# Moving LayerNorm, factor and block-sum steps inside a graph's turn, with shorter GpSimd chains for norms and scales

## The chip, the cores and the metric

The kernel runs on one core of a Trainium2 chip. The core has a matrix engine (TensorE, PE in the profile; its weight loads are PEld), a vector engine (VectorE, DVE), an activation engine (ScalarE, ACT), a general engine (GpSimd, POOL), and a queue that issues transfers (SyncE, SP). Each engine carries out its instructions in the order in which they were issued to it, and waits on semaphores for the others. TensorE's results go into PSUM, which the kernel uses as eight banks of 128 x 512 float32.

The metric is the device time of one execution in microseconds (us), median over the runs.

## The reference

64 graphs of 256 nodes with 256 features each, `x`, and a 256 x 256 adjacency with self loops, `adj`. Two layers, everything in float32:

```python
# layer 0
h   = relu(bn2(conv17(relu(bn1(conv1(x.T))))) + x.T).T    # along the nodes: a 1-tap and a 17-tap convolution
s   = x @ w_se.T + b_se                                   # 3 numbers for each node
A   = exp(-(|s_n|^2 + |s_m|^2 - 2 s_n.s_m)) * adj
nmp = A @ relu(x @ w_msg.T + b_msg)
gi, gh = concat(h, nmp) @ w_ih.T + b_ih, x @ w_hh.T + b_hh
r, z = sigmoid(gi_r + gh_r), sigmoid(gi_z + gh_z)
n   = tanh(gi_n + r * gh_n)
x   = layernorm(x + (1 - z) * n + z * x)
# layer 1
h   = layernorm(x) * gamma + beta
x   = layernorm(x + x + relu(adj @ h @ W_rel + b_rel + h @ W_root))
```

## The kernel before, in words

**Two streams of work.** The 17-tap convolution is done for eight graphs at once (a batch; eight batches) as a polynomial product in a transformed domain. Almost all of it is VectorE butterflies on one large buffer `XF` (lines 105, 302, 304, 362, 466), with 256-column products on TensorE between (`ps_k`, line 385) and, at the start of a batch, transposes and the 1-tap convolution (`ps_xTc`, `ps_c1`). It is written as a Python generator, `conv(b)`. The rest is done graph by graph: one pass of the inner loop, called a turn here, works on graph `k` and, for stages that run ahead or behind, on its neighbours.

**The order is written out by hand.** Nothing reorders instructions: the order of the calls is the order on every engine. At ten points of each turn `pump()` issues a portion of the *next* batch's convolution, in proportion to the number of points passed. So the convolution's VectorE and TensorE instructions lie between the turn's own. The last batch has no convolution beside it.

**A turn for graph k before the change**, in order, `|` being a pump:

- `gates` step 1: `ps_a` (block product 0) copied by ScalarE to `g00` (line 668), `ps_d` (product 1) added by VectorE (L671), a bias added by GpSimd (L672) |
- step 2: `ps_b` (product 4) copied by ScalarE to `g11` (L676), `ps_c` (product 6) added (L679); then ScalarE's last step for the `y` of graph k-2 (L793) and its store |
- `transposes_h(k-1)`: TensorE transposes `h` (L752), ScalarE copies to `hT` with gamma and beta (L754) |
- step 3: product 5 accumulates on `ps_a`, VectorE adds it (L682), GpSimd adds `g01` to `g11` (L684); the loads for later graphs |
- step 4: product 2 on `ps_b`, VectorE adds (L687), ScalarE tanh (L689); `passing(k+1)`: `ps_nmp`, copied by ScalarE (L630) |
- step 5: product 3 on `ps_c`, VectorE adds (L692), ScalarE tanh (L693); GpSimd `sums` for graph k+1 (below); `factors(k+2)`: TensorE transposes `st` (`ps_sT`, L604), ScalarE writes `lr` (L606, L607); `gates_n`: `ps_n`, added by VectorE (L704) |
- `project(k-1)`: `ps_out` from `hT` (L765), copied to `hr` (L766); `update` step 1: the two `gn` operations on VectorE, tanh (L717) |
- `distances(k+2)`: `ps_dist` from `lr` (L616), exp into `AT` (L618); `update` step 2: three VectorE operations on `x`, statistics (L708, L709), and a GpSimd chain for scale and shift (`q`, `sh`, L729 to L734, with a power of -1/2) |
- `messages(k+3)`: `ps_msg` (L584), two VectorE additions for each half (L586 into `st`, L588 into `msg`), ScalarE relu (L589), a GpSimd chain for the squared norms (L593 to L597); `update` step 3: ScalarE writes `h` and `x1` (L740, four instructions) |
- `mask(k+2)` (L621), `aggregate(k-1)` (L777, L779), VectorE statistics of `y`, a GpSimd chain (L787 to L790) |

**Block products.** The gates are one Strassen-like product of 2 x 2 blocks with seven products. Three left sides take part, `nmp`, `x` and `xc` (the convolution's output); each needs four 128 x 128 sums and differences, which `blocks` issues on GpSimd (L638 to L641). For the first graph of a batch the `xc` sums can only be issued when the whole convolution of that batch has been: they stand behind the loop over the eight graphs.

**Buffers.** `g`, `gn`, `h`, `hT`, `lr` and the sums have one buffer each, `AT`, `msg`, `nmp` and `y` two, `x` three, `xT` and `adj` four. PSUM banks go round through all eight, convolution and turn together.

Of the kernel before, what the change touches and what calls it, by code (L numbers as in the profile page):

```python
# [12 lines left out]
F32 = mybir.dt.float32  # L13
AF = mybir.ActivationFunctionType
ALU = mybir.AluOpType
# [14 lines left out]
BG = 8  # L30
# [47 lines left out]
def gnn_two_layers(  # L78
# [498 lines left out]
    def messages(k):  # L577
        MSG[k] = work.tile([P, C, D], F32, tag="msg", name="msg")
        st = sts[k % len(sts)]
        twice = st.rearrange("p m (r e) -> p m r e", e=SR)  # L580
        for m in range(C):
            ps = bank("ps_msg")
            for c in range(C):
                nc.tensor.matmul(ps[:, :D + 4], XT[k][:, c, m * P:(m + 1) * P], wms[:, c, :],  # L584
                                 start=(c == 0), stop=(c == C - 1))
            nc.vector.tensor_add(twice[:, m, :, 0:3], ps[:, D:D + 3].unsqueeze(1).to_broadcast([P, 2, 3]),  # L586
                                 bse_row.unsqueeze(1).to_broadcast([P, 2, 3]))
            nc.vector.tensor_add(MSG[k][:, m, :], ps[:, :D], bmsg)  # L588
# [43 lines left out]

    def blocks(src, s1, s2, s3, s4):

        a11, a12, a21, a22 = (src[:, c, n * P:(n + 1) * P] for n in range(C) for c in range(C))
        nc.gpsimd.tensor_add(s1, a21, a22)  # L638
        nc.gpsimd.tensor_sub(s2, s1, a11)
        nc.gpsimd.tensor_sub(s3, a11, a21)  # L640
        nc.gpsimd.tensor_sub(s4, a12, s2)  # L641
        return a11, a12, s4, a22, s1, s2, s3

    def sums(k, name):
# [8 lines left out]
        LEFT[k, name] = blocks(src, t[:, 0, :], t[:, 1, :], s3, t[:, 2, :])  # L653
# [57 lines left out]
    def update(k):  # L711

        g, w, nn = G[k], XG[k], GN[k]
        parts = nn.rearrange("p n (h e) -> p n h e", h=2)
        stt(nn, g[:, :, 0, :2 * P], 1.0, nn, op0=ALU.add, op1=ALU.mult)
        stt(parts, parts, 0.5, g[:, :, :, 2 * P:])
        nc.scalar.activation(nn, nn, AF.Tanh)  # L717
        yield

        nc.vector.tensor_sub(w, w, nn)  # L720
        stt(w, g[:, :, 1, :2 * P], 3.0, w, op0=ALU.add, op1=ALU.mult)
        stt(w, nn, 4.0, w)
# [12 lines left out]
        yield  # L735

        H[k] = work.tile([P, C, D], F32, tag="h", name="h", bufs=1)
        for i, dst in ((1, H[k]), (0, w)):
            for n in range(C):
                nc.scalar.activation(dst[:, n, :], w[:, n, :], AF.Identity,  # L740
                                     bias=sh[:, i, n:n + 1], scale=q[:, i, n:n + 1])
        X1[k] = w
        yield
# [60 lines left out]
    with tc.tile_pool(name="first", bufs=1) as first_pool:  # L804
# [34 lines left out]
                nc.sync.dma_start(out=t, in_=rows[:, src + at:src + at + n].to_broadcast([P, n]))  # L839
        bn_ = const.tile([P, D], F32)  # L840
        nc.sync.dma_start(out=bn_, in_=rows[:, R_HH + 2 * D:R_HH + 3 * D].to_broadcast([P, D]))
        gb = const.tile([P, 2, C], F32)
        nc.sync.dma_start(out=gb, in_=rows[:, R_GAMMA:R_GAMMA + 2 * D].rearrange("o (v c p) -> p (o v) c", p=P, c=C))

# [12 lines left out]
        nc.vector.tensor_add(bg[:, :, :2 * P], bg[:, :, :2 * P], bhh)  # L857
        nc.gpsimd.tensor_scalar(wrr, wrr, 0.5, None, ALU.mult)
        nc.gpsimd.tensor_scalar(brel, brel, 0.5, None, ALU.mult)
        while STAGE.get(0) != "inverse":  # L860
            total += next(first) or 0.0

# [30 lines left out]
            early.pop(0)()  # L893
    for f in early:
        f()
    sums(0, "xc")

    POINTS = 10
    y_left = None
    for b in range(NB):  # L900
        coming = conv(b + 1) if b + 1 < NB else iter(())
        done, at, goal = 0.0, 0, BG * POINTS - 6
# [9 lines left out]

        for k in range(b * BG, (b + 1) * BG):
            ga, up = gates(k), update(k)
            agg = None
# [12 lines left out]
            pump()  # L928
            step(ga)
            if k + 1 < B:  # L930
                passing(k + 1)
            pump()
            step(ga)
            if k + 1 < B:
                sums(k + 1, "x")
                if (k + 1) % BG:
                    sums(k + 1, "xc")
                sums(k + 1, "nmp")
            if k + 2 < B:
                factors(k + 2)  # L940
            gates_n(k)
            pump()
            if k > 0:
                project(k - 1)
            step(up)
            pump()
            if k + 2 < B:
                distances(k + 2)
            step(up)
            pump()  # L950
            if k + 3 < B:
                messages(k + 3)
            step(up)
            pump()
            if k + 2 < B:
                mask(k + 2)
            if k > 0:
# [58 lines left out]
```

## Time and profile before

| | |
|---|---|
| time, median of 3 runs | 2332.06 us (2329.61 to 2332.12) |
| span of the profiled execution | 2327.1 us, mean granted TensorE clock 0.979 |
| TensorE matmuls, busy | 2150.1 us, 92% |
| TensorE weight loads, busy | 1485.2 us, 64% |
| VectorE, busy | 1807.1 us, 78% |
| GpSimd, busy | 1044.0 us, 45% |
| ScalarE, busy | 872.0 us, 37% |

The first 188 us prepare the filters and the first batch's convolution; then come 64 turns. Busy shares are means over the whole span. The page also draws them in 40 slices, one digit for a tenth; the two rows that matter most here, TensorE's and VectorE's, differ strongly from slice to slice. "Idle before" in a group of instructions is the time in which its engine had nothing to do just ahead of them, and "<-" names what ended that. A wait named on an engine costs time only in a stretch in which that engine is the one that is behind.

### The profile page before, as it was taken

Reading aid. Unit: us, or ns where it says so; the run is one execution under the profiler, and the core shown is the slowest. Engines: PE = TensorE matmul, PEld = TensorE weight load, DVE = VectorE, ACT = ScalarE, POOL = GpSimd, SP = SyncE. Lnnn points to the kernel's source line nnn. Section 1 sums busy time; section 2 is a strip of 40 time slices with the busy share of each in tenths; the row PEclk is TensorE's granted clock in tenths of the full one; section 3 lists DMA queues with packets and bytes.
Section 4 is the critical chain, followed back from the end, with each engine's and each line's share of the span. In section 5 each row is a group of like instructions: output and inputs, shape, how many; then the busy total and the mean of one; then the engine's idle time right before and its main releaser. Section 6 shows DMA issues by size and latency. Waiting matters only on the chain.

```text
span 2327.1 us, 25882 instructions
## 1 busy us (share of the span) xinstructions
PE 2150.1 (92%) x8390; PEld 1485.2 (64%) x8390; DVE 1807.1 (78%) x3212; ACT 872.0 (37%) x1809; POOL 1044.0 (45%) x1829
## 2 busy tenths in 40 slices
PE   7877899999999999999999999999899999999997
PEld 4564577656766566665776567765676666766664
DVE  3992999849996699948998399975999579994454
ACT  4513322443235422353234532244323533235443
POOL 1004544537345453544436273453644545364542
PEclk9989999999999999999999999999999999999998
DMA  5543233222522234132332224222341214321110
GB/s 162 169 156 108 69 125 104 89 84 74 166 68 83 89 127 140 61 108 70 124 119 91 77 73 153 79 86 91 108 151 64 90 65 149 118 73 46 41 33 18
DMA packets 213939, 226.77 MB, mean 97 GB/s; under 512 B 22327, under 2 KB 205614, under 8 KB 213806
## 3 DMA queue, kind: packets, MB, share of 16 engines
q1 hardware_dynamic: 191248, 191.14, 25.9%
q10 hardware_dynamic: 22558, 33.99, 4.0%
q8 instruction: 68, 1.11, 0.2%
q14 instruction: 65, 0.53, 0.1%
HBM read 179.22 MB, written 45.88 MB: 97 GB/s over the span
## 4 chain that ended last, share of the span: by engine, by line
PE 42%; DVE 40%; issue 6%; POOL 5%; ACT 3%; DMA 3%; SPq 0%; ACTq 0%; POOLq 0%; DVEq 0%
DVE XF L105 12%; PE ps_k L385 7%; PE ps_c L657 5%; PE ps_b L657 5%; PE ps_a L657 4%; DVE XF L362 4%; PE ps_c L456 4%; DVE x L105 3%; PE ps_n L701 3%; PE ps_nmp L628 3%; DVE bst L708 3%; PE ps_out L765 2%; DVE XF L466 2%; PE ps_out L777 2%; DVE gn L105 2%
## 5 line engine op out<-in xcount | busy, mean ns | idle before, releaser
L105 DVE SCALAR_TENSOR_TENSOR XF<-XF 128x512 f32<-128x512 f32 (+2 forms) x800 | 572.4, 743 | 6.8
L385 PE MATMUL ps_k<-w,XF 128*128 128x256 f32 x1316 | 300.1, 383 | 12.2 <-ACT AT L618 11.6
L385 PEld LDWEIGHTS ps_k<-w,XF 128*128 128x128 f32 x1316 | 248.4, 191 | 61.7 <-ACT AT L618 17.3
L684 POOL TENSOR_TENSOR g<-g 128x384 f32<-128x384 f32 x64 | 79.6, 1243 | 397.6 <-DVE g L682 397.6
L729 POOL TENSOR_SCALAR q<-mv 128x2 f32<-128x2 f32 x64 | 32.2, 504 | 483.2 <-DVE mv L709 483.2
L765 PE MATMUL ps_out<-wrr,hT 128*128 128x512 f32 x512 | 231.8, 596 | 2.1 <-ACT hT L754 2.1
L589 ACT ACTIVATE msg<-msg 128x512 f32<-128x512 f32 x64 | 40.4, 631 | 370.5 <-DVE msg L588 370.5
L765 PEld LDWEIGHTS ps_out<-wrr,hT 128*128 128x128 f32 x512 | 97.8, 191 | 101.1 <-issue 86.5
L689 ACT ACTIVATE g<-g 128x512 f32<-128x512 f32 x64 | 40.5, 633 | 304.5 <-DVE g L687 303.3
L584 PE MATMUL ps_msg<-wms,xT 128*128 128x260 f32 x512 | 136.7, 408 | 8.1 <-DVE XF L401 4.7
L362 DVE TENSOR_TENSOR XF<-XF 128x512 f32<-128x512 f32 (+3 forms) x128 | 134.7, 1074 | 1.8
L456 PE MATMUL ps_c<-xTc,w 128*128 128x512 f32 x256 | 118.3, 605 | 9.7 <-ACT xTc L448 9.7
L628 PE MATMUL ps_nmp<-AT,msg 128*128 128x256 f32 x512 | 122.8, 383 | 1.1 <-DVE AT L621 1.1
L584 PEld LDWEIGHTS ps_msg<-wms,xT 128*128 128x128 f32 x512 | 95.6, 196 | 42.0 <-issue 19.4
L777 PE MATMUL ps_out<-hr,adj 128*128 128x256 f32 x512 | 121.9, 380 | 0.1
L701 PE MATMUL ps_n<-wn,xT 128*128 128x256 f32 x512 | 121.1, 379 | 0.0
L657 PE MATMUL ps_b<-wg,xcsum 128*128 128x384 f32 x256 | 105.1, 492 | 16.9 <-POOL xcsum L638 16.9
L628 PEld LDWEIGHTS ps_nmp<-AT,msg 128*128 128x128 f32 x512 | 98.3, 192 | 28.8 <-issue 1.8
L754 ACT ACTIVATE hT<-ps_hT,gb 128x256 f32<-128x256 f32 x128 | 65.0, 558 | 123.9 <-PE ps_hT L752 110.6
L682 DVE TENSOR_TENSOR g<-ps_a,bg 128x768 f32<-128x768 f32 x64 | 61.0, 952 | 64.8 <-PE ps_a L657 64.8
L657 PE MATMUL ps_b<-wg,nmpsum 128*128 128x384 f32 x256 | 106.1, 497 | 3.6 <-DVE y L779 2.3
L692 DVE TENSOR_TENSOR g<-g,ps_c 128x384 f32<-128x384 f32 x64 | 35.0, 547 | 95.7 <-PE ps_c L657 95.7
(150 smaller groups left out, 4918.5 us busy)
## 6 DMA issues: line engine op xcount, KB each, us to landing
w<-w2m SPq DMA_DIRECT2D x105, 768.0 KB, 4.8
xn<-in_x_dram SPq DMA_DIRECT2D x32, 512.0 KB, 4.6
xt<-xTc ACTq DMA_DIRECT2D x32, 512.0 KB, 4.7
xT<-xt SPq DMA_DIRECT2D x64, 256.0 KB, 3.9
adj<-in_adjT_dram SPq DMA_DIRECT2D x64, 256.0 KB, 2.7
x<-in_x_dram SPq DMA_DIRECT2D x64, 256.0 KB, 2.8
xb<-in_x_dram SPq DMA_DIRECT2D x32, 512.0 KB, 3.8
out_dram<-y ACTq DMA_DIRECT2D x64, 256.0 KB, 2.2
```

What stands on the lines that cost most here:

```text
L105: nc.vector.scalar_tensor_tensor(o, in0, s, in1, op0=op0, op1=op1)
L362: (nc.vector.tensor_add if add else nc.vector.tensor_sub)(sl(o, n), sl(a, n), sl(b, n))
L385: nc.tensor.matmul(ps, X[:, slot, c * P:(c + 1) * P], w(m, c), start=(c == 0), stop=(c == C - 1))
L456: nc.tensor.matmul(ps, w1[:, c, o * P:(o + 1) * P], xTc[:, c, :], start=(c == 0), stop=(c == C - 1))
L584: nc.tensor.matmul(ps[:, :D + 4], XT[k][:, c, m * P:(m + 1) * P], wms[:, c, :], start=(c == 0), stop=(c == C - 1))
L628: nc.tensor.matmul(ps[:, d * N:(d + 1) * N], MSG[k][:, m, d * P:(d + 1) * P], AT[k][:, m, :], start=(m == 0), stop=(m == C - 1))
L657: nc.tensor.matmul(ps[:, :w.shape[-1]], LEFT[k, name][i], w, start=start and j == 0, stop=j == 2, skip_group_check=not start)
L684: nc.gpsimd.tensor_add(g11, g11, g01)
L701: nc.tensor.matmul(ps[:, n * D:(n + 1) * D], XT[k][:, c, n * P:(n + 1) * P], wn[:, c, :], start=(c == 0), stop=(c == C - 1))
L708: nc.vector.bn_stats(st, src)
L765: nc.tensor.matmul(ps, hT[:, c, n * P:(n + 1) * P], wrr[:, c, :], start=(c == 0), stop=(c == C - 1))
L777: nc.tensor.matmul(po, ADJ[k][:, m, n * P:(n + 1) * P], hr[:, m, :], start=False, stop=(m == C - 1), skip_group_check=True)
```

## The change

Four things are changed, and the results stay the same up to rounding:

1. **Squared norms** (`messages`): two small VectorE instructions with an accumulated output give `-|s|^2` directly; of GpSimd's five instructions one is left.
2. **Scales** (`update`): one GpSimd addition of a constant tile `eps2` takes the place of two instructions; a factor goes into gamma once, at the start.
3. **Order in the turn**: `h` and `x1` (`update` step 3) are issued in the next turn, after its gates step 1 (`up_left`); `transposes_h(k-1)` goes from before step 3 to after step 4; `factors(k+2)` from after step 5 to before step 4; the `x` and `xc` sums from after step 5 to after step 4, the `nmp` sums to just behind `passing`, and `passing` and step 5 lie behind one pump more.
4. **Block sums at a batch's start**: the first graph's four `xc` sums are issued on VectorE and not on GpSimd.

```diff
@@ messages
+        ns = work.tile([P, C], F32, tag="ns", name="ns", bufs=3)
+        sq = work.tile([P, C, 3], F32, tag="sq", name="sq")
+        for m in range(C):
+            nc.vector.scalar_tensor_tensor(sq[:, m, :], st[:, m, 0:3], -1.0, st[:, m, 0:3], op0=ALU.mult,
+                                           op1=ALU.mult, accum_out=ns[:, m:m + 1])
         nc.scalar.activation(MSG[k], MSG[k], AF.Relu)
-        sq = work.tile([P, C, 3], F32, tag="sq", name="sq")
-        ns = work.tile([P, C], F32, tag="ns", name="ns", bufs=3)
-        nc.gpsimd.tensor_mul(sq, st[:, :, 0:3], st[:, :, 0:3])
-        nc.gpsimd.tensor_add(ns, sq[:, :, 0], sq[:, :, 1])
-        nc.gpsimd.tensor_add(ns, ns, sq[:, :, 2])
-        nc.gpsimd.tensor_scalar(twice[:, :, :, 3], ns.unsqueeze(2).to_broadcast([P, C, 2]), -0.5, None, ALU.mult)
-        nc.gpsimd.tensor_scalar(ns, ns, -1.0, None, ALU.mult)
+        nc.gpsimd.tensor_scalar(twice[:, :, :, 3], ns.unsqueeze(2).to_broadcast([P, C, 2]), 0.5, None, ALU.mult)
@@ update
-        nc.gpsimd.tensor_scalar(q[:, 0, :], mv[:, :, 1], 4 * EPS, None, ALU.add)
-        nc.gpsimd.tensor_scalar(q[:, 1, :], mv[:, :, 1], 1 + EPS, 4 * EPS * EPS, ALU.mult, ALU.add)
+        nc.gpsimd.tensor_tensor(q, mv[:, :, 1].unsqueeze(1).to_broadcast([P, 2, C]), eps2, ALU.add)
@@ before the loop, and behind each batch
-    sums(0, "xc")
+    sums(0, "xc", nc.vector)
...
-            sums((b + 1) * BG, "xc")
+            sums((b + 1) * BG, "xc", nc.vector)
@@ the turn
             step(ga)
+            step(up_left)
             pump()
             step(ga)
             step(y_left)
             pump()
-            if k > 0:
-                transposes_h(k - 1)
+            step(ga)
             pump()
-            step(ga)
-            load(k + 3)
-            load_adj(k + 2)
-            load_x(k + 1)
-            pump()
-            step(ga)
-            if k + 1 < B:
-                passing(k + 1)
-            pump()
+            if k + 2 < B:
+                factors(k + 2)
             step(ga)
             if k + 1 < B:
                 sums(k + 1, "x")
                 if (k + 1) % BG:
                     sums(k + 1, "xc")
+            load(k + 3)
+            load_adj(k + 2)
+            load_x(k + 1)
+            pump()
+            if k > 0:
+                transposes_h(k - 1)
+            pump()
+            if k + 1 < B:
+                passing(k + 1)
                 sums(k + 1, "nmp")
-            if k + 2 < B:
-                factors(k + 2)
+            step(ga)
             gates_n(k)
             pump()
...
             if k + 3 < B:
                 messages(k + 3)
-            step(up)
             pump()
...
-            y_left = agg
+            y_left, up_left = agg, up
```

More of the change, by code (lines that the diff above doesn't have):

```diff
@@ L630, in passing, with blocks, sums @@
         nc.scalar.copy(NMP[k].rearrange("p c n -> p (c n)"), ps)
-    def blocks(src, s1, s2, s3, s4):
+    def blocks(src, s1, s2, s3, s4, eng):
         a11, a12, a21, a22 = (src[:, c, n * P:(n + 1) * P] for n in range(C) for c in range(C))
[L638 to L641, printed above, removed]
+        eng.tensor_add(s1, a21, a22)
+        eng.tensor_sub(s2, s1, a11)
+        eng.tensor_sub(s3, a11, a21)
+        eng.tensor_sub(s4, a12, s2)
         return a11, a12, s4, a22, s1, s2, s3
-    def sums(k, name):
+    def sums(k, name, eng=None):
         if name == "x":
@@ L652, in sums @@
             s3 = src[:, 0, P:]
-        LEFT[k, name] = blocks(src, t[:, 0, :], t[:, 1, :], s3, t[:, 2, :])
+        LEFT[k, name] = blocks(src, t[:, 0, :], t[:, 1, :], s3, t[:, 2, :], eng or nc.gpsimd)
     def block_product(k, i, ps, start):
@@ L841, in gnn_two_layers @@
         nc.sync.dma_start(out=bn_, in_=rows[:, R_HH + 2 * D:R_HH + 3 * D].to_broadcast([P, D]))
+        eps2 = const.tile([P, 2, C], F32)
+        nc.gpsimd.memset(eps2[:, 0, :], 4 * EPS)
+        nc.gpsimd.memset(eps2[:, 1, :], 4 * EPS * EPS / (1 + EPS))
         gb = const.tile([P, 2, C], F32)
@@ L859, in gnn_two_layers @@
         nc.gpsimd.tensor_scalar(brel, brel, 0.5, None, ALU.mult)
+        nc.gpsimd.tensor_scalar(gb[:, 0, :], gb[:, 0, :], (1 + EPS) ** -0.5, None, ALU.mult)
         while STAGE.get(0) != "inverse":
@@ L895, in gnn_two_layers @@
         f()
-    sums(0, "xc")
+    sums(0, "xc", nc.vector)
     POINTS = 10
-    y_left = None
+    y_left = up_left = None
     for b in range(NB):
@@ L914, in gnn_two_layers @@
             ga, up = gates(k), update(k)
-            agg = None
             step(ga)
+            step(up_left)
             pump()
@@ L956, in gnn_two_layers @@
                 mask(k + 2)
+            agg = None
             if k > 0:
@@ L965, in gnn_two_layers @@
         if b + 1 < NB:
-            sums((b + 1) * BG, "xc")
+            sums((b + 1) * BG, "xc", nc.vector)
+    step(up_left)
     step(y_left)
```

## The prediction

> **What bounds the kernel now.** I read the page's busy shares and slices, then TensorE's waits, then a table of windows with one row for each turn of a batch, then VectorE's waits in a part of it, and last the timeline of one turn. TensorE looks like the bound (92%), but the slices of the two engines move against each other:
>
> ```profile
> PE   7877899999999999999999999999899999999997
> ...
> DVE  3992999849996699948998399975999579994454
> ```
>
> Of TensorE's own waits, longest in total first, these are the ones that the change touches:
>
> ```profile
> engine line waited for: us in total, times, longest us
> PE ps_hT L752 <- ACT h L740: 28.2, 42, 5.5
> PE ps_dist L616 <- ACT lr L607: 25.8, 25, 2.5
> ...
> PE ps_b L657 <- POOL xcsum L638: 16.9, 8, 5.3
> PE ps_a L657 <- ACT g L668: 16.4, 21, 0.8
> ```
>
> Together 87.3 us, 3.7% of the time. Whether they are worth that is read from the second batch (turns 8 to 15), one row a turn: length, then busy time of TensorE, weight loads, VectorE, ScalarE, GpSimd, the granted clock and the DMA.
>
> ```profile
> core 0: us, PE busy (x) PEld busy (x) DVE busy (x) ACT busy (x) POOL busy (x), PEclk, DMA share, GB/s
> 470.60:513.80 43.20, 41.54 (x158) 25.60 (x157) 16.23 (x25) 22.48 (x45) 13.89 (x34) 1.00 0.30 104
> 513.80:541.30 27.50, 24.68 (x94) 16.28 (x93) 26.17 (x39) 9.88 (x21) 19.09 (x28) 1.00 0.12 38
> 541.30:568.90 27.60, 24.67 (x93) 16.28 (x92) 27.12 (x48) 9.88 (x21) 18.72 (x27) 1.00 0.34 115
> 568.90:617.50 48.60, 45.38 (x189) 34.30 (x188) 46.08 (x83) 12.61 (x26) 19.79 (x40) 1.00 0.43 141
> 617.50:658.50 41.00, 39.97 (x165) 29.82 (x164) 37.87 (x73) 10.84 (x24) 15.65 (x27) 1.00 0.43 135
> 658.50:687.00 28.50, 28.30 (x113) 20.10 (x112) 28.05 (x55) 10.49 (x24) 13.85 (x22) 1.00 0.13 38
> 687.00:716.50 29.50, 27.30 (x102) 18.03 (x101) 28.76 (x50) 10.12 (x22) 19.86 (x28) 0.94 0.30 99
> 716.50:744.30 27.80, 26.95 (x118) 18.81 (x116) 15.19 (x33) 16.71 (x37) 11.91 (x25) 1.00 0.23 75
> ```
>
> The first and the last turn are TensorE's: it idles 1.66 and 0.85 us, VectorE 27.0 and 12.6. The six between have VectorE busy for 194.05 of 202.70 us. There TensorE's waits for `h`, `lr` and `g` are only where it stands while VectorE is behind. What holds VectorE in that stretch (window 508 to 721, which takes in the end of the first turn):
>
> ```profile
> engine line waited for: us in total, times, longest us
> DVE gn L704 <- PE ps_n L701: 2.1, 2, 1.4
> DVE XF L466 <- ACT XF L459: 1.8, 1, 1.8
> DVE g L692 <- PE ps_c L657: 1.0, 1, 1.0
> DVE g L687 <- POOL g L684: 0.9, 1, 0.9
> DVE g L671 <- ACT g L668: 0.8, 1, 0.8
> ```
>
> So a batch is two parts in a row. VectorE's runs from the first turn's late `XF` (L466, which waits for TensorE's 1-tap convolution) to the `y` of the seventh; TensorE's from there (its `ps_b` waits 0.6 us for that `y`, L779, for a bank) through the next batch's first turn. The last batch is TensorE's alone: in the window 2100 to 2290 its only listed wait is one of 1.7 us for `xcsum`.
>
> [...] here a 128x128 sum took 0.45 us on GpSimd when undisturbed, and VectorE's 128x256 took 0.41, so with half the columns VectorE should need about 0.28 (0.68 for 512, 0.41 for 256: 0.27 for each 256, and half of that less).
>
> **Part by part.**
>
> *Sums on VectorE at a batch's start.* TensorE waits 5.3 us once and 1.66 us at each of seven batch starts. At 470 to 477 us GpSimd ends the norm chain, the squared norms and the `y` chain at 476.50 before it starts `xcsum` (476.46 to 476.91); TensorE could have begun at 475.31. VectorE ends its statistics at 474.78 and is then idle until 475.58: the first sum ends near 474.78 + 0.28 + 0.3 (norms, below) = 475.4. The wait falls to about 0.1: 7 x 1.5 = 10.5 us. The other three sums delay L671 by some 0.4 us, in a stretch where VectorE has 27 us to spare. At the first turn GpSimd's sums stood behind 128x768 weight sums of 1.8 us each; on VectorE, idle there from 186.7 to 192.7, they stand behind nothing: 5.3 us. The wait of 1.33 us for `nmpsum` just before goes too, as the GpSimd queue loses four small instructions ahead of it (0.19, 0.19, 0.20 and 1.09 us): 1.3 us.
>
> *`h` and `x1` in the next turn.* Four ScalarE instructions of 0.59 us, 2.36 in all, no longer stand before the copy of `g00`. TensorE loses its 16.4 us of waits, and VectorE its 0.8 us at L671 in the fourth turn of a batch and 1.5 in turn 1. Only VectorE's part counts: 7 x 0.8 + 1.5 = 7.1 us. Now `g11`'s copy stands behind them, but its bank is complete 5.4 us after `ps_a` (two products of 2.7), so it isn't late; and GpSimd's `sh` is finished before the next turn's first copy in the saturated turns (520.50 against 522.52).
>
> *Transposes and factors.* `h` and `lr` are ready long before their readers, so the 28.2 and 25.8 us vanish from the list. I count nothing for that in VectorE's turns, because a new wait takes their place: `hT`'s copies now stand behind the tanh of step 4 on ScalarE, which waits for VectorE's L687. In the turn at 513.8 TensorE without waits would reach `ps_out` at about 531; L687 ends near 530.8 by my estimate (one pump earlier than its 532.8), and tanh (0.63) and two copies (1.02) put `hT` at 532.5. TensorE then waits about 1.5 us at `ps_out`, with hr, distances and messages behind it. The bank wait of `ps_hT` for the convolution (`XF` L401, up to 1.9 us in the fourth turn) passes to a later allocation, behind step 3's 1.9 us: TensorE is earlier at that turn's `ps_n`, where VectorE waits 0.7. I take 0.5 us a batch: 3.5. In the fifth turn VectorE's waits for `ps_c` and `ps_n` (1.0 + 1.4) only change shares, for the TensorE work up to `ps_n` is the same. L687 still has one pump between it and L682, so its wait for GpSimd (0.9) shrinks by 0.3 at most, where that pump is longer: 7 x 0.3 = 2.1.
>
> *Shorter GpSimd chains.* L593 to L595, L597 and one of L729/L730 go: mean durations 369 + 328 + 220 + 307 + 259 ns, 95 us of GpSimd over 64 turns, at 45% use and with no reader waiting except as above. Nothing.
>
> *Norms on VectorE.* Two instructions, four with the accumulator reads, for each turn, on the engine that is behind. The nearest rows are L586 (128x6, mean 151 ns, yet the next starts only 0.07 us after it) and L709 (182 ns). Lower end: two starts of 0.07, 0.15 us a turn. Upper end: four of 0.15, 0.6 us. I take 0.3, four starts of 0.07. They lie in VectorE's part 7 times a batch, in 7 batches: 49 x 0.3 = +14.7 us (7.4 to 29.4). In TensorE's turns VectorE's idle time hides them.
>
> Sum: -10.5 - 5.3 - 1.3 - 7.1 - 3.5 - 2.1 + 14.7 = -15.1, so 2332.1 - 15.1 = 2317.0 us.
>
> **Rivals.**
>
> *A, TensorE's waits come off the clock.* For: TensorE is busy for 92% and the four waits are 87.3 us. In full that gives 2244.8. Against: VectorE in its six turns has just 8.65 us to give in a batch. If TensorE's lead took half of that, 7 x 4.3 = 30 us, in place of the 7 x 1.6 that I count, the time would be 2317.0 - 30 + 11.2 = 2298.
>
> *B, the norms eat it all.* For: the added instructions stand on the saturated engine, and the earlier sums let GpSimd's 128x128 operations lie beside more of VectorE's butterflies: in the turn at 513.8 a sum took 1.43 us where it takes 0.45 alone, and butterflies of 128x512, median 0.68, average 0.77. With 0.6 us a turn the sum is -15.1 + 14.7 = -0.4; with 0.2 us a saturated turn of such contention (42 turns) besides, +8: 2340, slower. Against: statistics instructions of like size go by at 0.1 us from start to start (L709 to the next L708).
>
> *C, new waits end the gain.* VectorE's L682 comes one pump earlier after L679; its slack was 1.8 us in the fifth turn. If it waits 1 us in three turns of each batch that is +21 less what later waits shrink by (about half): 2327, no change.
>
> **How the numbers follow.** My forecast 0.55 (2305 to 2327), A in part or in full 0.17, no change through B or C 0.15, slower 0.13. The likeliest gives 2317. From 2297 (A's half) to 2333 (B's upper end and a little contention) leaves out about 0.07 below and 0.11 above. Faster 0.55 + 0.17 = 0.72; same 0.15; slower 0.13.
>
> **What would show it.** Right: `xcsum` gone from TensorE's waits or near 0.1 us; no more waits for `h`, `lr` and `g` L668, but `ps_out` waiting for `hT` with 20 us or more in total; the middle six turns with VectorE's busy share unchanged, and 0.15 to 0.6 us more of it a turn. Wrong: lengths of those six turns falling by over 3 us a batch (then TensorE's lead counted), or growing (then the norms or GpSimd's contention cost more), or TensorE's first turns losing less than 1 us.

## The result, and the profile after

| | before | after |
|---|---|---|
| time, median | 2332.09 us | 2354.65 us (4 runs, 2352.38 to 2354.84) |
| ratio | 1 | 1.0096, 95% interval 1.0079 to 1.0114 |
| span of the profiled execution | 2327.1 us | 2352.7 us |

The changed kernel is slower by 22.6 us, where 15 us of gain was forecast. In its listing the lines from about L600 on are one lower than before (L687 of before is L686, L692 is L691, L765 is L764).

The slices of TensorE and VectorE on the page of after:

```profile
PE   7878899999999999998999999999999999999997
...
DVE  3994999759896799949998499975989679895454
```

The two still change places, so a batch is still VectorE's part and TensorE's part in a row. TensorE's longest waits in after (us in total, times, longest):

```profile
PE ps_out L764 <- ACT hT L753: 56.2, 28, 3.3
PE ps_k L385 <- DVE g L686: 21.3, 14, 1.9
...
PE ps_b L656 <- ACT g L675: 14.4, 21, 1.2
...
PE ps_k L385 <- ACT XF L400: 10.1, 7, 2.1
```

The waits for `h`, for `g` at L668 and for `xcsum` are gone or small, as foreseen, and `ps_out` waits for `hT`, as foreseen. Not foreseen are the wait of `ps_b` for `g` at L675 (the copy of `g11`, which now stands behind `h` and `x1`) and the two of `ps_k`: it waits for a PSUM bank that VectorE's step 4 (L686), or ScalarE's L400, has still to read. The second batch by turns, in the columns of the table shown before:

```profile
core 0: us, PE busy (x) PEld busy (x) DVE busy (x) ACT busy (x) POOL busy (x), PEclk, DMA share, GB/s
467.70:510.40 42.70, 41.56 (x157) 25.77 (x157) 17.18 (x33) 22.63 (x45) 10.82 (x25) 1.00 0.31 105
510.40:537.30 26.90, 24.41 (x93) 16.19 (x92) 25.57 (x43) 9.77 (x21) 18.63 (x23) 1.00 0.12 39
537.30:567.70 30.40, 26.45 (x94) 16.75 (x93) 29.89 (x54) 10.31 (x22) 18.48 (x25) 0.94 0.32 104
567.70:616.50 48.80, 45.66 (x189) 34.20 (x188) 44.84 (x88) 12.38 (x25) 20.31 (x28) 1.00 0.44 141
616.50:661.30 44.80, 41.92 (x165) 30.91 (x165) 38.98 (x78) 11.28 (x24) 13.94 (x22) 0.96 0.39 123
661.30:690.10 28.80, 28.50 (x113) 20.03 (x113) 28.35 (x53) 9.83 (x22) 12.74 (x19) 1.00 0.12 37
690.10:722.10 32.00, 27.58 (x101) 17.49 (x101) 31.19 (x59) 10.94 (x24) 19.21 (x23) 0.95 0.29 98
722.10:748.60 26.50, 26.50 (x117) 18.81 (x116) 14.47 (x33) 16.72 (x37) 10.55 (x19) 1.00 0.22 72
```

The six middle turns grew from 202.70 to 211.70 us. VectorE's busy time in them went from 194.05 to 198.82, its idle time from 8.65 to 12.88: about half of the loss is more work or slower work on VectorE, half is VectorE standing (idle at a wait; such a stretch is called a stand below). It stands in the fifth turn above all (41.0 before, 44.8 now). VectorE's waits in the window 505 to 727 of after:

```profile
engine line waited for: us in total, times, longest us
DVE g L691 <- PE ps_c L656: 5.5, 2, 3.8
DVE gn L703 <- PE ps_n L700: 2.3, 2, 1.2
...
```

Before, L692 waited 1.0 us there. Over the six batches from the second to the seventh the mean lengths of the eight turns, worked out from the two traces at the first `ps_a` product of each turn, are:

| turn of a batch | 1 | 2 | 3 | 4 | 5 | 6 | 7 | 8 | sum |
|---|---|---|---|---|---|---|---|---|---|
| before | 43.9 | 27.2 | 28.3 | 48.1 | 41.0 | 28.5 | 30.3 | 27.2 | 274.5 |
| after | 42.4 | 27.8 | 28.4 | 49.8 | 44.0 | 28.8 | 31.7 | 26.7 | 279.5 |

In these means the six middle turns grow by 7.0 us a batch; VectorE's busy time is 3.9 of that and its idle time 3.1.

### The profile page after: what moved, and what is told of

Its sections match the earlier page's. It is cut to its first block, busy times and chain, and to the rows that moved or that the text cites. A ratio compares the mean times of both kernels' runs of the same rounds, so it can differ in the third digit from the quotient of the medians.

```text
span 2352.7 us, 25793 instructions
## 1 busy us (share of the span) xinstructions
PE 2159.4 (92%) x8390; PEld 1482.5 (63%) x8390; DVE 1845.6 (78%) x3500; ACT 877.3 (37%) x1809; POOL 971.1 (41%) x1480
## 4 chain that ended last, share of the span: by engine, by line
DVE 44%; PE 42%; issue 6%; POOL 3%; DMA 3%; ACT 2%; SPq 0%; ACTq 0%; DVEq 0%; POOLq 0%
DVE XF L105 16%; PE ps_k L385 7%; PE ps_c L656 5%; PE ps_a L656 5%; PE ps_c L456 4%; PE ps_out L764 4%; PE ps_b L656 3%; DVE XF L362 3%; PE ps_n L700 3%; DVE x L105 3%; DVE bst L707 3%; PE ps_nmp L627 3%; DVE XF L466 2%; PE ps_out L776 2%; PE ps_d L656 2%
## 5 line engine op out<-in xcount | busy, mean ns | idle before, releaser
L105 DVE SCALAR_TENSOR_TENSOR XF<-XF 128x512 f32<-128x512 f32 (+2 forms) x800 | 595.8, 773 | 6.5
L385 PE MATMUL ps_k<-w,XF 128*128 128x256 f32 x1316 | 307.9, 388 | 43.1 <-DVE g L686 21.3
L764 PE MATMUL ps_out<-wrr,hT 128*128 128x512 f32 x512 | 256.3, 648 | 56.2 <-ACT hT L753 56.2
L729 POOL TENSOR_TENSOR q<-mv,eps 128x4 f32<-128x4 f32 x64 | 31.3, 489 | 537.5 <-DVE mv L708 293.9
L764 PEld LDWEIGHTS ps_out<-wrr,hT 128*128 128x128 f32 x512 | 103.2, 206 | 178.5 <-issue 96.6
L691 DVE TENSOR_TENSOR g<-g,ps_c 128x384 f32<-128x384 f32 x64 | 35.1, 549 | 174.6 <-PE ps_c L656 174.6
L656 PE MATMUL ps_b<-wg,nmpsum 128*128 128x384 f32 x256 | 106.0, 496 | 16.1 <-ACT g L675 14.4
L792 ACT ACTIVATE y<-y,sh,q 128x256 f32<-128x256 f32 x128 | 69.9, 594 | 134.6 <-POOL sh L789 133.9
L700 PEld LDWEIGHTS ps_n<-wn,xT 128*128 128x128 f32 x512 | 97.3, 190 | 26.9
L776 PEld LDWEIGHTS ps_out<-hr,adj 128*128 128x128 f32 x512 | 96.4, 190 | 15.9 <-ACT hr L765 1.6
```

The lines of the kernel that those rows point to most:

```text
L105: nc.vector.scalar_tensor_tensor(o, in0, s, in1, op0=op0, op1=op1)
L385: nc.tensor.matmul(ps, X[:, slot, c * P:(c + 1) * P], w(m, c), start=(c == 0), stop=(c == C - 1))
L656: nc.tensor.matmul(ps[:, :w.shape[-1]], LEFT[k, name][i], w, start=start and j == 0, stop=j == 2, skip_group_check=not start)
L700: nc.tensor.matmul(ps[:, n * D:(n + 1) * D], XT[k][:, c, n * P:(n + 1) * P], wn[:, c, :], start=(c == 0), stop=(c == C - 1))
L764: nc.tensor.matmul(ps, hT[:, c, n * P:(n + 1) * P], wrr[:, c, :], start=(c == 0), stop=(c == C - 1))
L776: nc.tensor.matmul(po, ADJ[k][:, m, n * P:(n + 1) * P], hr[:, m, :], start=False, stop=(m == C - 1), skip_group_check=True)
```

## The experiments

All ratios are to the kernel before, run beside each on the same chip; one per cent is 23.3 us.

| run | what it is | median us | ratio, 95% interval |
|---|---|---|---|
| e1 | before + new order only | 2374.88 | 1.0183 (1.0167 to 1.0199) |
| e2 | after with the old order | 2309.48 | 0.9903 (0.9888 to 0.9918) |
| e3 | before + transposes and pump moved | 2404.55 | 1.0316 (1.0298 to 1.0334) |
| e4 | after, norms on GpSimd again | 2345.78 | 1.0058 (1.0042 to 1.0075) |
| e5 | before + pump moved | 2360.95 | 1.0119 (1.0104 to 1.0134) |
| e6 | before + transposes moved | 2388.70 | 1.0224 (1.0193 to 1.0254) |
| e7 | before + sums on VectorE | 2310.22 | 0.9899 (0.9884 to 0.9914) |
| e8 | after with the old pumps | 2368.41 | 1.0146 (1.0127 to 1.0165) |
| e9 | e6, bank of `hT` taken early | 2387.42 | 1.0225 (1.0204 to 1.0246) |
| e10 | e6, copies into `hT` before the tanh | 2334.50 | 1.0002 (0.9991 to 1.0013) |
| e11 | after, transposes at the old place | 2338.10 | 1.0019 (1.0007 to 1.0030) |
| e12 | e2 + `h`, `x1` in the next turn | 2316.11 | 0.9923 (0.9907 to 0.9939) |
| e13 | before without GpSimd's sums | 2275.79 | 0.9762 (0.9747 to 0.9777) |
| e14 | e5 without GpSimd's sums | 2291.38 | 0.9824 (0.9811 to 0.9838) |
| e15 | after, copies before the tanh | 2335.21 | 1.0012 (1.0005 to 1.0020) |
| e16 | e8, copies before the tanh | 2333.51 | 1.0006 (0.9999 to 1.0013) |
| e17 | after, `ps_nmp` ahead of the pump | 2333.57 | 1.0000 (0.9992 to 1.0008) |
| e18 | e16, gap filled with repeated products | 2320.37 | 0.9946 (0.9933 to 0.9959) |

**Which part is it? e1, e2, e4, e7.** Theory 1: the order in the turn costs the time. Theory 2: the norms on VectorE cost it.

e1 takes only the turn of the changed kernel, without the other three parts:

```diff
+            step(up_left)
...
-            if k > 0:
-                transposes_h(k - 1)
+            step(ga)
             pump()
-            step(ga)
...
```

> The kernel before with the new order of the turn alone (h and x1 in the next turn, transposes, factors and sums at their new places; norms, scales and the batch-start sums stay on GpSimd). Theory 1 (the order costs it: with one pump more ahead of step 5, the convolution's products stand before a PSUM bank that VectorE's L686 must free, and VectorE then waits for ps_c): 2355 to 2370 us, as the changed kernel but without its gain of some 15 us at the batch starts. Theory 2 (the norms on the saturated VectorE cost it): 2325 to 2335 us.

e2 is its complement, the changed kernel with the turn of before:

```diff
-            if k + 2 < B:
-                factors(k + 2)
...
+            if k > 0:
+                transposes_h(k - 1)
...
```

> The changed kernel with the old order of the turn: norms on VectorE, one GpSimd scale instruction less, batch-start sums on VectorE. Theory 1: 2320 to 2328 us (the batch starts give 15 to 17, the norms cost 0.17 us in 49 turns, 8). Theory 2: 2345 us or more.

e4 puts the five GpSimd instructions for the norms back into the changed kernel:

```diff
-            nc.vector.scalar_tensor_tensor(sq[:, m, :], st[:, m, 0:3], -1.0, st[:, m, 0:3], op0=ALU.mult,
-                                           op1=ALU.mult, accum_out=ns[:, m:m + 1])
+        nc.gpsimd.tensor_mul(sq, st[:, :, 0:3], st[:, :, 0:3])
...
```

> The changed kernel with the squared norms on GpSimd again, as before. Theory 1: 2343 to 2350 us (8 us less than the changed kernel's 2354.7). Theory 2: 2325 to 2335 us.

e7 takes the block sums alone:

```diff
-            sums((b + 1) * BG, "xc")
+            sums((b + 1) * BG, "xc", nc.vector)
```

> The kernel before with the batch-start sums on VectorE and nothing else. Both theories: 2312 to 2318 us, as the waits for xcsum (16.9 us) go. If it is 2310 or less, the norms on VectorE cost the kernel with the old order nothing; at 2301 they cost the 8 us that they cost with the new order.

The order costs 42.7 us (e1), the sums bring 23.6 (e7), the norms cost 8.9 (after against e4, an interval of some 3 to 14 us). Together +28.0 where +22.6 was measured: they add up within their intervals. Theory 1 holds, theory 2 accounts for less than half of the loss. With the old order the norms and shorter chains together change nothing that can be measured (0.9903 against 0.9899).

**Which move of the order? e3, e5, e6, e8, e11, e12.** e5 moves one pump, so that steps 3 and 4 come earlier; e6 moves the transposes behind step 4; e3 does both:

```diff
# e5
             if k > 0:
                 transposes_h(k - 1)
+            step(ga)
             pump()
             step(ga)
             load(k + 3)
...
             pump()
-            step(ga)
+            pump()
             if k + 1 < B:
                 passing(k + 1)
-            pump()
# e6
-            if k > 0:
-                transposes_h(k - 1)
             pump()
...
             step(ga)
+            if k > 0:
+                transposes_h(k - 1)
             if k + 1 < B:
                 passing(k + 1)
```

> The kernel before with one move: step 3 follows step 2 after one pump, and transposes_h with its pump goes behind step 4, so that passing and step 5 lie behind one pump more. Theory 1: this move is the harmful one, 2350 to 2370 us, with waits of ps_k for g L687 in two turns of each batch. Theory 2, or another part of the order at fault: within 5 us of 2332.

> The kernel before with one pump moved: the one between transposes_h and step 3 now stands behind the pump after step 4, ahead of passing and step 5; transposes_h stays ahead of step 3. Theory 1a (the place of the pump does the harm: two portions of the convolution now stand ahead of step 5, their products need the banks of step 3 and 4 back from VectorE, and VectorE later waits for ps_c): 2375 to 2410 us, with 20 us or more of ps_k waiting for g L687. Theory 1b (the place of the transposes does it, through hT's copies behind the tanh): within 6 us of 2332.

> The kernel before with transposes_h moved from before step 3 to after step 4, every pump at its old place. Theory 1a: 2325 to 2338 us. Theory 1b: 2370 us or more, with waits of ps_out for hT.

Each alone costs, the transposes twice as much as the pump (+52 and +28), and both about their sum (+74). The whole new order costs less than these two moves of it (43 us, e1); which of its other moves gives the difference back was not tested. e8 and e11 undo one of the two in the changed kernel (e8 also puts GpSimd's sums back behind step 5), e12 takes `h` and `x1` in the next turn as the only move:

```diff
# e8: pumps as before, transposes behind step 4
+            pump()
             step(ga)
...
# e11: transposes before step 3, pumps as after
+            if k > 0:
+                transposes_h(k - 1)
             step(ga)
             pump()
# e12
+            step(up_left)
...
-            step(up)
```

> The changed kernel with its pumps at their old places: h and x1 in the next turn, factors ahead of step 4, transposes_h after step 4, norms and batch-start sums on VectorE; sums after step 5 as before. Theory 1a: 2300 to 2312 us, below the 2309.5 of the changed kernel with the old order or equal to it. Theory 1b: 2345 us or more.

> The kernel after with nothing but the transposes put back before step 3 (pumps, factors, h and x1, sums, norms as after). If the place of the transposes is the main harm (e6: +55 of order's +43 with the helping moves): 2310 to 2325. If the pump placement is the main harm (e5: +27 by itself): 2335 to 2350.

> All that helps: block sums on VectorE, norms, eps2, and of the turn's order only h and x1 issued in the next turn; transposes, pumps and factors at their old places. My step for h and x1 in the prediction says -7 against e2 (2309.5): 2302. If TensorE's waits for h stand only where VectorE is behind and L671's wait is made up elsewhere: 2308 to 2311. If the later h runs into the transposes before step 3 (TensorE then waits for h at ps_hT with 1 us in each turn): 2315 to 2335.

e8 is slower than the changed kernel itself, so the old pumps do not help while the transposes stand behind step 4. With the transposes back (e11) the changed kernel loses 18 us of its time. The +4 us that are left are fewer than what pump, norms and sums leave by themselves (28 + 9 - 24 = 13). The move of `h` and `x1` brings nothing: e12 stands 0.2% above e2, with intervals that touch.

**What the moved pump costs: e13, e14.** In e5 VectorE's butterflies take longer, although their number is the same. Two of their groups by form, first in the kernel before, then in e5 (busy us, mean ns):

```profile
L105 DVE SCALAR_TENSOR_TENSOR XF<-XF 128x512 f32<-128x512 f32 x448 | 334.3, 771 | 5.0
...
L302 DVE TENSOR_TENSOR XF<-XF 128x256 f32<-128x256 f32 x112 | 46.5, 416 | 0.2
```

```profile
L105 DVE SCALAR_TENSOR_TENSOR XF<-XF 128x512 f32<-128x512 f32 x448 | 350.4, 808 | 5.0
...
L302 DVE TENSOR_TENSOR XF<-XF 128x256 f32<-128x256 f32 x112 | 53.5, 478 | 0.2
```

The changed kernel has the same lengthening:

```profile
L105 DVE SCALAR_TENSOR_TENSOR XF<-XF 128x512 f32<-128x512 f32 x448 | 348.9, 805 | 5.0
```

With the old order (e7) this group takes 770 ns. Theory contention: GpSimd's 128x128 sums now lie beside these butterflies. Both runs leave GpSimd's block sums out; the products take plain blocks, so the gates are not those of the reference:

```diff
-        nc.gpsimd.tensor_add(s1, a21, a22)
-        nc.gpsimd.tensor_sub(s2, s1, a11)
-        nc.gpsimd.tensor_sub(s3, a11, a21)
-        nc.gpsimd.tensor_sub(s4, a12, s2)
-        return a11, a12, s4, a22, s1, s2, s3
+        return a11, a12, a12, a22, a21, a22, a21
```

> The kernel before without GpSimd's block sums: the products take plain blocks of nmp, x and xc as their left sides, so the gates are not the reference's; everything else is as before. It is the base for the next run. Without xcsum at the batch's start at least the 22 us of e7 go: 2295 to 2312; if GpSimd's sums slow VectorE's butterflies in the kernel before too, lower still, 2270 to 2295.

> The same omission in the kernel of e5 (one pump behind step 4, 2361 us, +27 over before). Theory contention: with the pump there, GpSimd's 128x128 sums lie beside VectorE's small butterflies, which take longer (128x512, 128x256: +42 us in e5's trace by their summed durations, part of it in overlap); without sums the moved pump costs nothing, so the time is within 6 us of the run without sums on the kernel before. Theory order: the pump's place itself makes VectorE or TensorE late; the distance stays at 20 us or more.

The distance fell from 28 us to 14.5 (0.62%, with intervals of about 0.14% on each ratio), between what the two theories said; the turns tell them apart. The middle six grow by 4.1 us a batch from before to e5 (203.5 to 207.6), and by nothing from e13 to e14 (199.9 and 199.8). VectorE's busy time in them grows by 5.8 us a batch from before to e5 (194.6 to 200.4), and by 0.3 from e13 to e14 (189.1 to 189.4). The first turn, which is TensorE's, grows by 1.8 and still by 1.1. The same two groups in e13 and in e14:

```profile
L105 DVE SCALAR_TENSOR_TENSOR XF<-XF 128x512 f32<-128x512 f32 x448 | 319.9, 739 | 5.0
...
L302 DVE TENSOR_TENSOR XF<-XF 128x256 f32<-128x256 f32 x112 | 46.5, 415 | 0.2
```

```profile
L105 DVE SCALAR_TENSOR_TENSOR XF<-XF 128x512 f32<-128x512 f32 x448 | 321.1, 743 | 5.0
...
L302 DVE TENSOR_TENSOR XF<-XF 128x256 f32<-128x256 f32 x112 | 46.4, 414 | 0.2
```

Without the sums the moved pump slows neither. (Not every group does so: the 256 butterflies of 128x256 at L105 went from 471 to 492 ns, and the 48 of 128x512 at L302 from 799 to 683; together VectorE's work is as long.) (In the kernel before the sums cost time too: e13 is 56 us faster, and only 24 of that are the wait that e7 takes away.) So in VectorE's turns the pump's cost is contention, and in the first turn it is something else: `ps_c` of the 1-tap convolution waits for ScalarE's `xTc` for 16.9 us in e5 and 9.7 before, and without the sums for 16.7 in e14 and 8.5 in e13. (In three batches of e5 L687 also waits 5.5 us for `xsum`, all in the first turn.) Not all of VectorE's instructions take longer in e5: its additions to `msg` (L588), with one input in PSUM, took 415 ns on average before and 413 in e5. What the two engines contend for, the traces do not show.

**What the moved transposes cost: e9, e10.** Theory bank order: `hT`'s PSUM bank, taken later, leaves a bad one to `ps_k`. Theory tanh: ScalarE's copies into `hT` stand behind the tanh of step 4.

```diff
# e9
+            ps_h = bank("ps_hT") if k > 0 else None
...
-                transposes_h(k - 1)
+                transposes_h(k - 1, ps_h)
# e10: step 4 ends before its tanh, which is issued behind the copies
         nc.vector.tensor_add(g01, g01, b_[:, :HG])
+        yield
...
                 transposes_h(k - 1)
+            step(ga)
```

> The kernel with the transposes behind step 4 (e6, 2388.7 us), but their PSUM bank is taken at the old place, before step 3, so that all later buffers fall on the banks that they had before. Theory bank order: moving the transposes moves the bank of hT in the round, ps_k in the fourth turn of a batch then gets a bank that VectorE frees late (L401, waits of 3.2 us), runs at half rate behind it, and L692 stands 4.6 us; with the bank at its old place these waits go and the time is 2330 to 2350. Theory tanh: the loss is that hT's copies stand behind the tanh of step 4 on ScalarE, with ps_out and all behind it late; the copies stand there still, so the time stays at 2375 to 2392.

> e6 again (2388.7 us), but ScalarE gets the two copies into hT ahead of the tanh of step 4; TensorE's order and the bank order are those of e6. Theory tanh: TensorE's waits for hT (34.4 us) go, 2335 to 2360. Theory bank order: those waits go from the list, but the fourth turn's waits of ps_k for L401 stay and with them the time, 2375 to 2392.

e10 took the whole 52 us back. e9 turned out to be no test: its main waits are e6's (`ps_k` for L401 33.8 us in both), so asking for the bank earlier did not change which release the later products wait for. (The description of the kernel says that the banks go round; if they simply did, e9 should have given the later products their old banks. How they are picked stays open.) But e10 doesn't confirm the tanh theory as it was put either. Two of TensorE's waits in e6, and its only listed wait of `ps_k` for VectorE in e10:

```profile
PE ps_out L765 <- ACT hT L754: 34.4, 21, 2.7
PE ps_k L385 <- DVE XF L401: 33.8, 14, 3.2
```

```profile
PE ps_k L385 <- DVE g L682: 5.9, 4, 2.1
```

Both waits of e6 are gone with one move on ScalarE, although TensorE and VectorE have the same order in the two kernels. In e6 the time is lost where `ps_k` waits: the fourth turn grew by 4.4 us and the fifth by 1.9, and VectorE's L692 waits 4.6 and 3.0 us there. (In the fourth turn of the second batch `ps_k` stands 3.19 us, and the 16 records behind it take 5.41 us.) (The sixth grew by 1.6 too, with VectorE busy.) The waits for `hT` lie in the second, sixth and seventh turns, where VectorE hardly stands. Which of the two waits costs the time is what e15 and e17 had to tell.

**Inside the changed kernel: e15, e17.** e15 is the changed kernel with the copies ahead of the tanh. e17 moves only TensorE's `ps_nmp` and its copy:

```diff
# e17
                 transposes_h(k - 1)
-            pump()
             if k + 1 < B:
                 passing(k + 1)
+            pump()
+            if k + 1 < B:
                 sums(k + 1, "nmp")
```

> The kernel after (2354.65 us) with one difference: ScalarE gets the two copies into hT ahead of the tanh of step 4. If ScalarE's order carries the transposes' harm, as in e10 against e6, the waits of ps_out for hT (56.2 us) go and the time falls to what is left of the pump's +27 less the gain of the sums: 2320 to 2340. If the harm in after is the pump alone, 2348 to 2356.

> The kernel after (2354.65 us), with ps_nmp back ahead of the pump behind the transposes; GpSimd's nmp sums, step 5 and all else stay. Theory stand: in the fourth and fifth turns TensorE now reaches the third ps_k too early (1.2 and 1.85 us before VectorE's L686 frees its bank), stands, and comes late to ps_c, for which VectorE's L691 then stands (1.7 and 3.0 us a turn); ps_nmp's 1.7 us lay in that gap in the kernel before. Back there it fills the gap: the fifth turn falls from 44.0 to about 41, the fourth by about 1, 2322 to 2338. If the pump's contention and hT behind the tanh carry the loss: 2347 to 2358.

Each takes 20 to 22 us off, and each makes the fifth turn shorter (41.0 and 42.5 us for 44.0). In e15 the fourth turn becomes longer (53.2 for 49.8), with a stand of `ps_k` for L400 like the one of e16 below; in e17 it becomes shorter by 1.6. e17 settles which wait it is: `ps_out` waits for `hT` for 56.2 us in e17 as in after, and `ps_k` for L686 only 9.3 us in place of 21.3 and for L400 5.7 in place of 10.1. TensorE in the fifth turn of the second batch, before, after, and in e17:

```profile
633.46 1.89 PE L628 MATMUL ps_nmp<-AT,msg 128*128 128x256 f32 x8
635.19 5.34 PE L385 MATMUL ps_k<-w,XF 128*128 128x256 f32 x24
640.37 0.81 PE L657 MATMUL ps_c<-wg,nmp 128*128 128x384 f32 x2
```

```profile
632.70 1.89 PE L385 MATMUL ps_k<-w,XF 128*128 128x256 f32 x8
636.44 5.41 PE L385 MATMUL ps_k<-w,XF 128*128 128x256 f32 x16 [1.85 <-DVE g L686]
641.69 1.89 PE L627 MATMUL ps_nmp<-AT,msg 128*128 128x256 f32 x8
643.41 0.81 PE L656 MATMUL ps_c<-wg,nmp 128*128 128x384 f32 x2
```

```profile
629.86 1.89 PE L627 MATMUL ps_nmp<-AT,msg 128*128 128x256 f32 x8
631.59 1.03 PE L385 MATMUL ps_k<-w,XF 128*128 128x256 f32 x4
633.61 4.86 PE L385 MATMUL ps_k<-w,XF 128*128 128x256 f32 x20 [0.99 <-DVE g L686]
638.30 0.81 PE L656 MATMUL ps_c<-wg,nmp 128*128 128x384 f32 x2
```

The same work stands in all three. Before, the 1.7 us of `ps_nmp` passed while VectorE was still on its way to the bank that `ps_k` needs. In after `ps_nmp` lies behind, TensorE stands 1.85 us, and then needs 5.41 us for 16 records (the trace has two for each matmul here: eight matmuls more in e18, below, are 16 records more), where 24 took 5.34 us before. The clock that the trace shows as granted is 0.50 for 3.41 us of that, from 636.87 on, and 1.00 throughout in the `ps_k` lines of before and of e17. VectorE in after pays for both:

```profile
635.85 0.54 DVE L686 TENSOR_TENSOR g<-g,ps_b 128x384 f32<-128x384 f32 x1
...
645.34 0.56 DVE L691 TENSOR_TENSOR g<-g,ps_c 128x384 f32<-128x384 f32 x1 [3.81 <-PE ps_c L656]
```

In e17 this wait of L691 is 1.24 us.

The second batch is one of three that pay for both. The fifth turn of after has the stand of 1.85 us in all seven batches with a convolution beside them, but the half clock follows it in three only:

| fifth turn | its length | L691 (L692) waits |
|---|---|---|
| before, 7 batches | 41.0 | 1.1 |
| after, 4 batches, full clock | 43.1 | 2.1 |
| after, 3 batches, half clock | 44.8 | 3.8 |
| e17, 7 batches | 42.5 | 1.2 |

So the stand alone costs VectorE 1.1 us of waiting, and the half clock 1.7 more where it comes. In the fourth turn L691 waits 1.66 us in each batch of after, at full clock, and not at all before.

**Is it the stand, or the rate after it? e16, e18.** e16 was meant to take both harms out, pumps at their old places and copies first. It has no wait for `hT`, yet in its fourth turn `ps_k` stands 4.27 us for a bank that ScalarE's L400 frees. e18 adds work to exactly that gap (lines behind it move: L404 of e18 is L400, and L692 of e16 and L696 of e18 are L691 of after):

```diff
             product(p2[:, at], re + k, w, 1)
+            if k == 0:
+                for _ in range(4 if FILL[0] == 1 else 0):
+                    product(p2[:, at], re + k, w, 1)
+                FILL[0] -= 1
```

> e8 (2368 us: after's parts with the pumps at their old places, factors before step 4, h and x1 in the next turn, transposes behind step 4) with ScalarE's copies into hT ahead of the tanh. If hT behind the tanh was all of e8's loss: 2300 to 2312, below e7's 2310 if h, lr and g issued early are worth anything. If moving the transposes costs by itself: 2335 or more.

> e16 (2333.5 us) with work added: in the fourth turn of each batch, where ps_k stands 4.2 us for a bank that ScalarE's L400 frees, TensorE repeats the product before it four times (eight more matmuls of 128x256, about 3.5 us, the same result written again). Theory clock: the long stand puts TensorE at half its rate for about 3.4 us afterwards (16 matmuls take 5.41 us in place of 3.72), so that ps_c comes late for VectorE's L692 (2.6 us a turn); with the gap filled it keeps its rate, L692's stand falls by about 1.7 us in 7 turns and the time to 2316 to 2326, although work was added. Theory stand: the bank comes when it comes and the rate after it is hidden; 2330 to 2338.

Eight more matmuls in each of seven turns made the kernel 13 us faster (1.0006 to 0.9946). TensorE's `ps_k` in that turn, in e16 and in e18:

```profile
570.04 7.10 PE L385 MATMUL ps_k<-w,XF 128*128 128x256 f32 x32
581.41 5.41 PE L385 MATMUL ps_k<-w,XF 128*128 128x256 f32 x16 [4.27 <-ACT XF L400]
```

```profile
564.35 10.60 PE L385 MATMUL ps_k<-w,XF 128*128 128x256 f32 x48
575.77 3.72 PE L385 MATMUL ps_k<-w,XF 128*128 128x256 f32 x16 [0.83 <-ACT XF L404]
```

The bank comes no earlier (18.3 us after the turn's first product in e16, 18.4 in e18); what changed is that the 16 records behind it take 3.72 us and not 5.41. The granted clock over them is 0.68 in e16 (0.50 for 3.41 us of it) and 1.00 in e18, and so it is in all seven batches: half clock behind that stand in e16, none in e18. VectorE's wait for `ps_c` in that turn went from 2.35 to 0.66 us, the same 1.69 us:

```profile
599.59 0.55 DVE L692 TENSOR_TENSOR g<-g,ps_c 128x384 f32<-128x384 f32 x1 [2.35 <-PE ps_c L656]
```

```profile
592.26 0.56 DVE L696 TENSOR_TENSOR g<-g,ps_c 128x384 f32<-128x384 f32 x1 [0.66 <-PE ps_c L660]
```

So this stand costs VectorE time by the rate that follows it. Seven turns of 1.7 us are 12 of the 13 us. e18 is still 10 us above e7; its eighth turn is 4.6 us longer than in the kernel before (31.8 for 27.2). The fastest kernels of the study stay e2 and e7, the old order with the sums on VectorE, 1% below the kernel before; no move of the order improved on them.

## Why the prediction was wrong, by its steps

- **Where the bound lies**: right. The six middle turns are VectorE's, and what was lost was lost there; the first and last turns gained (1.4 and 0.5 us a batch). Rival A is out: TensorE's waits for `h` and `lr` all but went and those for `g` at L668 fell to 6.1 us, and the kernel became slower. The gain of the first turn is less than what the sums alone bring there (2.2 in e7).
- **Sums on VectorE** (-17.1): right and too small; e7 measured -23.6. (VectorE's 128x128 sums took 0.26 to 0.29 us each in most cases, as estimated.) The first turn of a batch fell by 2.2 us in place of 1.5, that of the first batch by 8.1 in place of 6.6.
- **`h` and `x1` in the next turn** (-7.1): no gain was measured (e12). The 0.8 us at L671 go from the list, and VectorE's part gets no shorter. The copy of `g11` was said not to be late because its bank is complete 5.4 us after `ps_a`; in the turn at 513.8 of before two products take 3.4 us, and `ps_b` waits for that copy for 14.4 us in after, all in turns where VectorE hardly stands.
- **Transposes and factors** ("I count nothing"; bank wait -3.5; L687 -2.1): this is the step that failed; its gain of 5.6 us was a loss. It looked for the cost in the wait of `ps_out` for `hT`, found 1.5 us, and set it against the waits that vanish. That wait came (56.2 us), but nearly all of it in the second, third and seventh turns, where VectorE idles as little as before (1.3, 0.5 and 0.8 us a turn in both traces); e17 keeps it and is 22 us faster. The loss came by two ways that the step left out.
  - The sentence that "in the fifth turn VectorE's waits for `ps_c` and `ps_n` (1.0 + 1.4) only change shares, for the TensorE work up to `ps_n` is the same": the work is the same, its order isn't. With `ps_nmp` behind the pump TensorE comes too early to a bank, stands 1.85 us, in three batches of seven goes on at half its rate, and is late for `ps_c`: VectorE's wait there grows by 1.8 us on average in the fifth turn and by 1.7 in the fourth. e17 undoes that one move: 22 us off, the fourth and fifth turns shorter by 3.0 us a batch, and VectorE's idle time in the middle turns back from 11.9 to 9.4 us (8.9 before).
  - The moved pump puts GpSimd's sums beside VectorE's butterflies (e5 against e14, 4.1 us a batch in the middle turns, nothing without the sums). In the changed kernel VectorE's instructions on `XF` in a batch's middle turns take 4.7 us more, summed (130.4 to 135.2), and still do in e17. Rival B named this contention, at 8 us, for the sums that come earlier; the prediction didn't ask what the moved pump does to it.
- **Norms on VectorE** (+14.7): mis-sized within its range. After against e4 gives +8.9; with the old order no cost was seen (e2 against e7). Four instructions a turn take 0.17 us from start to start, not 0.3: 49 x 0.17 = 8.3. That an accumulator read of its own comes with each was only assumed in the prediction (before has none on VectorE); the trace of after shows it, 0.09 us behind 0.16 or 0.17 us:

```profile
661.03 0.16 DVE L592 SCALAR_TENSOR_TENSOR sq<-st 128x3 f32<-128x3 f32 x1
661.11 0.09 DVE L592 DVE_READ_ACCUMULATOR sq<-st 128x1 f32 x1
661.11 0.17 DVE L592 SCALAR_TENSOR_TENSOR sq<-st 128x3 f32<-128x3 f32 x1
661.20 0.09 DVE L592 DVE_READ_ACCUMULATOR sq<-st 128x1 f32 x1
661.20 1.23 DVE L105 SCALAR_TENSOR_TENSOR XF<-XF 128x1024 f32<-128x1024 f32 x1
```

- **Shorter GpSimd chains** (nothing): agrees with e2 against e7.
- **Rival C** named a new wait of VectorE, and one came, but not where it looked: the wait for `ps_a` at L682 is 0.2 us in all middle turns of after together (none before), the one for `ps_c` at L691 31.5 us (7.4 before).

What stays open: how a PSUM bank is picked, and so why one move on ScalarE changes what `ps_k` waits for (e6 to e10); what GpSimd and VectorE contend for; why only some stands of one length have the half clock behind them; the 14.5 us that the moved pump costs without GpSimd's sums, of which the longer wait for `xTc` in the first turns is 8.2; what holds e18 above e7; and why the whole order costs less than two of its moves.

## What to carry to other kernels

When a reordering leaves the work of an engine the same, look for what used to pass the time in front of each wait on a buffer: an instruction moved from ahead of a wait to behind it turns hidden time into a stand, and the engine that is really the bound pays when it next reads (here 1.7 us of `ps_nmp` became a stand of 1.85 us, and VectorE's wait for `ps_c` in the fifth turn went from 1.1 to 2.1 us, or 3.8 with the half clock). The rule given ahead, that a wait costs time only on the engine that is behind, needs this added: TensorE is not behind in the middle turns, yet its stands there end in VectorE's waits. A total of waits says little: 56 us of them lie where VectorE's idle time stayed as it was, while e17, with 16 us less of others, is 22 us faster. So read each wait by the stretch it lies in and by who stands next. On GpSimd and VectorE, ask what a moved instruction will lie beside, not only what it waits for (448 butterflies went from 771 to 808 ns on average in e5).

## What was not expected of the hardware

**TensorE at half rate after many stands of 2 us and more.** In all twenty traces, from 190 us on, I counted stands of TensorE of over 0.3 us that at least five matmuls follow without a gap, and called the rate halved where three of the next eight took over 1.6 times the median of their form from start to start. After stands under 2 us that holds for 78 of 1349, between 2 and 2.5 us for 96 of 187, from 2.5 us on for 143 of 172. The granted clock agrees: it falls to 0.50 in 359 stretches, 261 of them 3.41 us long and most others two or three times that. The length of a stand alone does not decide: one of 1.85 us in the fifth turn of after is followed by the half clock in three batches and not in four. What does decide, the traces do not show. e18 shows what the half clock is worth: with the gap of 4.27 us down to 0.83 us the 16 records behind it take 3.72 us in place of 5.41, and the kernel is 13 us faster.

**Contention by placing alone.** The same 448 butterflies of 128x512 took 771, 805, 808, 739 and 743 ns on average in before, after, e5, e13 and e14.
